# A linear layer with 28 groups of 512 tokens, its weight sums kept for all tokens, and a third recursion level in three of seven products

## The chip, the cores and the metric

The kernel runs on one core of a Trainium2 chip. The metric is the device time of one execution in microseconds (us). Several executions are compared by their median.

## What is computed

Two layers, all in 32-bit floats, each added to its input. x has 32 sequences of 128 tokens and 2048 features.

```python
x = x + (x @ W.T + bias + scale[b] * ((x @ A[b].T) @ B[b].T))   # b = itok_B_1_7, rank 16, 8 adapters
x = x + x @ W1[c].T                                             # c = itok_B_1_14, per sequence, 2048 x 2048
```

The first layer has one weight for all 4096 tokens and a small low-rank term per sequence. The second has a weight per sequence, so that 32 weights of 16 MB are read.

## The kernel before

Both layers multiply by a recursion that replaces 8 products of half-size blocks by 7, at the price of sums of blocks (Strassen's scheme in Winograd's form). In each level the seven products need four sums of x's blocks (s1 to s4) and four of the weight's (t1 to t4), and the results are put together from sums U of the products.

The first layer uses two levels. `PHASES` (lines 21 to 41) writes out the outer one: phase i has a list of x's quarters that are added up, a list of w0's quarters that are added up, the names of an old partial result that it reads and of a new one that it writes ("P1", "U2", "U3", "U4", in DRAM), and for phases 3 to 6 the quarter of the output that becomes final. Within a phase, x is worked on in two groups of 1024 tokens, and w0 in four parts of 256 outputs: a unit is (phase, group, part), 56 in all. Each unit does the inner level: seven products of four matmuls each, 128 x 128 weights on 512 columns of x (`product`, lines 498 to 503, in the order 1, 2, 6, 5, 7, 3, 4), each into one of eight PSUM banks. The sums of w0 are made again for each group: `w_terms` adds the quarters up and `w_sums` makes the inner level's four, one unit ahead. `a_terms` and `a_sums` do the same for x, a group ahead.

All engines run in the order in which the program is written (`manual_schedule`, line 136). ScalarE copies product 1, 6, 5 and 7 out of PSUM, VectorE adds the rest (lines 647 to 691), and `finish` (line 542) adds the old partial result, stores the new one by POOL's queue, or, where the quarter is final, adds x itself (the residual) and the other partial and stores to `x1t`, the second layer's input, in DRAM. `Loads` (lines 45 to 69) hands out slots of one large SBUF tile, `mem`: a load that is in line begins when a slot of its pool is free, and SyncE's queue issues the loads in that order.

The low-rank term has two steps. `lowrank` multiplies x with the adapters' A (32 x 32-wide pieces, side by side in the array) while the quarters of x for phase 1 are in SBUF, and `lowrank_out` scales the result into `low`, with a 1 in an extra row for the bias. `add_low` (line 507) multiplies it with the adapters' B (`load_b`, on POOL's queue) and adds it into the banks of a unit that ends a quarter.

The second layer (lines 698 to 767) takes pairs of sequences and eight parts of the weight per pair, 128 steps n in all. `load_w1` loads two steps ahead, `sums_w1` makes the sums one step ahead (the identity that stands for the residual is added to the weight's diagonal), and seven products of four matmuls follow on 512 columns with 64 rows of tokens (line 732), the first into bank 7. The last unit of the first layer (`ends`, line 640) already loads and adds up for the second.

Of the kernel before, what the change touches and what calls it, by code (L numbers as in the profile page):

```python
# [41 lines left out]
LOW = 1  # L42


class Loads:


    def __init__(self, pools):
        self.free = {k: list(v) for k, v in pools.items()}
        self.todo = []  # L50
        self.held = {}

    def add(self, key, pool, begin):
        self.todo.append((key, pool, begin))

    def pump(self):
        while self.todo and self.free[self.todo[0][1]]:
            key, pool, begin = self.todo.pop(0)
            slot = self.free[pool].pop(0)
            self.held[key] = (pool, slot)  # L60
            begin(slot)
# [4 lines left out]
    def done(self, key):  # L66
        pool, slot = self.held.pop(key)
        self.free[pool].append(slot)
        self.pump()


@with_exitstack
def cond_resid_kernel(
# [55 lines left out]

    nc = tc.nc  # L130
    B, S, D = out.shape
    NW, _, _, _, P, _, _, NF = w1q.shape
    NA, _, _, _, RT, _ = bt.shape
# [10 lines left out]

    mem = const.tile([P, 21, 4 * NF], F32, tag="mem", name="mem")
# [6 lines left out]
    units = [(i, g, o) for i in range(len(PHASES)) for g in range(2) for o in range(4)]  # L152
    part = {
        (k, g, o): dram.tile([P, 4 * NF], F32, tag=f"{k}_{g}{o}", name=f"{k}_{g}{o}")
        for k in ("P1", "U2", "U3", "U4")
        for g in range(2)
        for o in range(4)
# [33 lines left out]
    homes = {"w": (0, 12, 4), "t": [8, 9, 10], "x": (), "s": []}  # L191
# [24 lines left out]
    def sums_w1(n):  # L216
# [14 lines left out]
        )  # L231
        sub(t1, b12, b11)
        sub(b12, b22, b12)
        sub(t2, b22, t1)
        w1s[n] = {1: b11, 2: b21, 3: b22, 4: t4, 5: t1, 6: t2, 7: b12}
        return lambda: sub(t4, b21, t2)
# [25 lines left out]
    with tc.tile_pool(name="c0", bufs=1) as c0, tc.tile_pool(  # L262
        name="ev", bufs=1
    ) as evp, tc.tile_pool(name="bs", bufs=2) as bsp:
        tset = c0.tile([P, 2, 3, 4, P], F32, tag="tset", name="tset")


        low = {
            (r, g): c0.tile([P, 4, S], F32, tag=f"low{r}{g}", name=f"low{r}{g}")
            for r in range(2)  # L270
            for g in range(2)
        }
        bank_a, bank_b, bank_c = ([bank[:, 2 * k + m] for m in range(2)] for k in range(3))
        bank_d, bank_l = banks_r = bank[:, 6], bank[:, 7]


        loads = Loads(
            {"A": range(8), "W": (13, 11, 12), "st": (17, 16, 15, 14, 18)}
        )

        def view(slot, *shape):
            names = "abcd"[: len(shape)]
            return mem[:, slot].rearrange(
                f"p ({' '.join(names)}) -> p {' '.join(names)}", **dict(zip(names[1:], shape[1:]))
            )

        def add_w(n):
            i, g, o = units[n]
            for k, (_, r, c) in enumerate(PHASES[i][1]):
                halves = (0,) if n == 0 else (slice(None),)  # L290
                loads.add(
                    ("W", n, k), "W" if k == 0 else "st",
                    lambda slot, src=w0q[r, c, o], halves=halves: load_w(slot, src, halves),
                )

        def load_w(slot, src, halves):
            for h in halves:
                nc.sync.dma_start(out=view(slot, 2, 2, 4, P)[:, h], in_=src[:, h])  # L298

        def first_a(slot, src):  # L300

            for i in range(2):
                nc.sync.dma_start(out=view(slot, 4, NF)[:, ts(i, 2)], in_=src[:, ts(i, 2)])  # L303
            _, r, c = PHASES[0][1][0]
            load_w(loads.slot(("W", 0, 0)), w0q[r, c, 0], (1,))

        def add_a(group, q):

            i, g = divmod(group, 2)
            t, h = divmod(q, 2)  # L310
            terms = [(r, k) for _, r, k in PHASES[i][0]]
            if i == LOW:
                terms += [(0, 1)]
                loads.add(("a", group, q), "st", lambda slot: load_a(slot, g, t, h))
            for m, (r, k) in enumerate(terms):
                loads.add(
                    ("A", group, q, m), "A" if m == 0 else "st",
                    (lambda slot, src=xq[r, g, t, k, h]: first_a(slot, src))
                    if group == q == 0
                    else lambda slot, src=xq[r, g, t, k, h]: nc.sync.dma_start(  # L320
                        out=view(slot, 4, NF), in_=src
                    ),
                )

        def early(n):

            return n < len(units) and PHASES[units[n][0]][4] and (
                PHASES[units[n][0]][3] or n % 2 == 1
            )

        def add_x(n):
            i, g, o = units[n]

            def load_x(slot):
                r, c, _ = PHASES[i][4]
                for t in range(2):
                    nc.sync.dma_start(
                        out=view(slot, 2, 2, NF)[:, t],
                        in_=xq[r, g, t, c, o // 2, :, ts(o % 2, 2)],
                    )  # L340

            loads.add(("x", n), "st", load_x)

        def add_end(n):
            i, g, o = units[n]
            _, _, old, new, final = PHASES[i]
            if early(n + 1):
                add_x(n + 1)
            if final and not early(n):
                add_x(n)  # L350
            for k in (old, final[2] if final else None):
                if k:
                    loads.add(
                        (k, n), "st",
                        lambda slot, k=k: nc.sync.dma_start(out=mem[:, slot], in_=part[k, g, o]),
                    )

        def load_a(slot, g, t, h):
            for r in range(2):
                for s in range(4):  # L360
                    n = adapter(id0_ok, 16 * r + 8 * g + 4 * t + s, NA - 1, POOL)
                    nc.gpsimd.dma_start(
                        out=view(slot, 2, 4, 8, RT)[:, r, s],
                        in_=at[ds(n, 1), h].rearrange("o p k i r -> (o p) (k i) r"),
                    )

        add_w(0)
        for q in range(2):
            add_a(0, q)
        add_w(1)  # L370
        for q in range(2, 4):
            add_a(0, q)
        for n in range(len(units)):
            if n // 4 + 1 < 2 * len(PHASES):
                add_a(n // 4 + 1, n % 4)
            if n + 2 < len(units):
                add_w(n + 2)
            add_end(n)
        loads.pump()


        for k in range(16):
            nc.tensor.matmul(bank_l[:, :P], lhsT=ident, rhs=ident, start=True, stop=True)

        id0_ok = clamped(id0_sb, NA - 1, "id0_ok")
        id1_ok = clamped(id1_sb, NW - 1, "id1_ok")
# [14 lines left out]
        scale = c0.tile([P, B // 4], F32, tag="scale", name="scale")  # L401


        def signed(sign, dst, src):
            (add if sign > 0 else sub)(dst, dst, src)

        def w_view(n):
            return view(loads.slot(("W", n, 0)), 2, 2, 4, P)

        def w_terms(n):  # L410

            for k, (sign, _, _) in enumerate(PHASES[units[n][0]][1]):
                if k:
                    signed(sign, mem[:, loads.slot(("W", n, 0))], mem[:, loads.slot(("W", n, k))])
                    loads.done(("W", n, k))

        def w_sums(n):

            w = w_view(n)
            t1, t2, t4 = (tset[:, n % 2, k] for k in range(3))  # L420
            sub(t1, w[:, 0, 1], w[:, 0, 0])
            sub(t2, w[:, 1, 1], t1)
            sub(w[:, 0, 1], w[:, 1, 1], w[:, 0, 1])
            sub(t4, w[:, 1, 0], t2)
            return {
                1: w[:, 0, 0], 2: w[:, 1, 0], 3: w[:, 1, 1], 4: t4, 5: t1, 6: t2, 7: w[:, 0, 1]
            }

        def a_terms(group, q):
            terms = PHASES[group // 2][0]  # L430
            dst = mem[:, loads.slot(("A", group, q, 0))]
            for m, (sign, _, _) in enumerate(terms):
                if m:
                    signed(sign, dst, mem[:, loads.slot(("A", group, q, m))])
                    loads.done(("A", group, q, m))
            if group // 2 == LOW:
                loads.done(("A", group, q, len(terms)))
# [104 lines left out]
        def finish(n):  # L542
# [4 lines left out]
            if new:  # L547
# [6 lines left out]
                if old:  # L554
                    loads.done((old, n))
# [282 lines left out]
```

## Time and profile before

| what | us |
|---|---|
| median of 3 runs | 2972.87 (2972.39 to 2975.28) |
| the profiled execution, its own time | 2974.56 |
| its span, first to last instruction | 2972.9 |
| first matmul of the first layer | 7.47 |
| first matmul of the second layer | 1429.81 |

The profile shows one execution. "Busy" is the time in which an engine had an instruction under way. PE is TensorE's matmuls and PEld its weight loads, DVE is VectorE, ACT is ScalarE, POOL is GpSimd, SP is SyncE. A group of instructions is told as line, engine, operation, output<-input, shapes and count, then busy time, mean ns of one, and the engine's idle time ahead of them with what ended it. The sums on VectorE carry the lines of two helpers, 178 (`add`) and 181 (`sub`). A 32-bit matmul of the program shows as two records. DMA issues are told with their size and the median time from issue to landing.

### The profile page before, as it was taken

The page shows a single profiled execution, that of the slowest core. Times are in us where ns is not written, and L with a number is a line of the kernel's source. Part 1 is how long each engine was busy: PE and PEld are TensorE (multiplying, and loading weights), DVE is VectorE, ACT ScalarE, POOL GpSimd, SP SyncE. Part 2 cuts the span into 40 slices and gives each one's busy share as a digit, 9 for nine tenths or more (in the row PEclk, how much of TensorE's full clock was granted, in tenths as well). Part 3 has the DMA queues.
Part 4 walks back from the last instruction along what each step waited for, and adds up shares of the span by engine and source line. Part 5 has one row for each costly group of instructions (what it writes and reads, how often), then busy time and mean ns, then how long its engine had stood idle before and what let it go on. Part 6 is the DMA issues. An engine that isn't in the chain of part 4 may idle for free.

```text
span 2972.9 us, 32939 instructions
## 1 busy us (share of the span) xinstructions
PE 2961.1 (100%) x12384; PEld 1174.1 (39%) x12384; DVE 2351.3 (79%) x1717; ACT 197.7 (7%) x340; POOL 239.1 (8%) x427
## 2 busy tenths in 40 slices
PE   9999999999999999999999999999999999999999
PEld 4445444444444444444333333333333333333333
DVE  3367755567645768874999999999999999999997
ACT  1111111111111111111000000000000000000000
POOL 1111000022212221221000000000000000000000
PEclk9999999999999999999999999999999999999999
DMA  5679866689975899986999999999999999999995
GB/s 226 241 308 357 344 264 255 258 298 346 363 262 210 325 346 377 367 348 234 372 399 383 397 384 406 389 400 388 399 391 396 388 383 408 390 395 387 405 388 222
DMA packets 186015, 1025.62 MB, mean 345 GB/s; under 512 B 23808, under 2 KB 23808, under 8 KB 79616
## 3 DMA queue, kind: packets, MB, share of 16 engines
q1 hardware_dynamic: 142512, 906.68, 77.1%
q0 software_dynamic: 25248, 83.92, 7.4%
q10 hardware_dynamic: 18096, 32.91, 3.5%
q8 instruction: 98, 1.61, 0.2%
q14 instruction: 61, 0.50, 0.0%
HBM read 922.76 MB, written 100.66 MB: 344 GB/s over the span
## 4 chain that ended last, share of the span: by engine, by line
PE 98%; DMA 1%; DVE 1%; issue 0%; SPq 0%; ACT 0%; DVEq 0%; ACTq 0%
PE bank L732 52%; PE bank L500 44%; PE bank L511 1%; PE bank L467 1%; DMA mem<-in_w0q_dram 0%; DMA mem<-in_xq_dram 0%; DVE mem L178 0%; DVE mem L181 0%; DVE tset L181 0%; SPq L303 0%; SPq L298 0%; DVE res L178 0%; ACT p L624 0%; ACT kept L524 0%; DVEq L178 0%
## 5 line engine op out<-in xcount | busy, mean ns | idle before, releaser
L181 DVE TENSOR_TENSOR mem<-mem 128x2048 f32<-128x2048 f32 (+1 forms) x733 | 1483.2, 2052 | 49.6 <-DMA mem<-in_w0q_dram 25.9
L732 PE MATMUL bank<-mem 128*64 128x512 f32 x5120 | 1120.7, 592 | 0.0
L500 PE MATMUL bank<-mem 128*128 128x512 f32 x1792 | 792.4, 595 | 3.1 <-DMA mem<-in_xq_dram 3.1
L732 PEld LDWEIGHTS bank<-mem 128*64 128x64 f32 x5120 | 367.9, 137 | 730.9 <-issue 692.7
L500 PE MATMUL bank<-mem,tset 128*128 128x512 f32 x1344 | 595.8, 593 | 2.5 <-ACT p L624 2.5
L500 PEld LDWEIGHTS bank<-mem 128*128 128x128 f32 x1792 | 340.3, 191 | 425.6 <-issue 420.1
L732 PE MATMUL bank<-mem,s 128*64 128x512 f32 x2048 | 461.2, 592 | 0.0
L178 DVE TENSOR_TENSOR mem<-mem 128x2048 f32<-128x2048 f32 (+2 forms) x195 | 338.9, 1750 | 100.2 <-ACT mem L691 49.0
L500 PEld LDWEIGHTS bank<-mem,tset 128*128 128x128 f32 x1344 | 255.1, 190 | 321.7 <-issue 318.3
L732 PEld LDWEIGHTS bank<-mem,s 128*64 128x64 f32 x2048 | 147.2, 137 | 292.3 <-issue 292.3
L178 DVE TENSOR_TENSOR mem<-u,p 128x512 f32<-128x512 f32 x56 | 38.6, 690 | 197.2 <-ACT u L660 197.2
L492 POOL DMA_DIRECT2D b_sel<-in_bt_dram x256 | 134.7, 526 | 341.7 <-PE bank L511 180.1
L738 ACT COPY pv<-bank 128x512 f32<-128x512 f32 x32 | 18.7, 586 | 1516.1 <-PE bank L732 1041.3
L178 DVE TENSOR_TENSOR pv<-bank,pv 128x512 f32<-128x512 f32 x64 | 44.2, 691 | 78.9 <-PE bank L732 77.9
L178 DVE TENSOR_TENSOR mem<-kept,mem 128x512 f32<-128x512 f32 x28 | 18.7, 690 | 106.4 <-ACT kept L524 106.4
L181 DVE TENSOR_TENSOR tset<-mem,tset 128x512 f32<-128x512 f32 x112 | 77.2, 689 | 7.7 <-PE bank L500 4.1
L178 DVE TENSOR_TENSOR mem<-mem,ident 128x1024 f32<-128x1024 f32 x64 | 78.1, 1220 | 0.0
L178 DVE TENSOR_TENSOR mem<-bank,u 128x512 f32<-128x512 f32 x56 | 38.5, 687 | 48.1 <-PE bank L500 48.1
L535 POOL DMA_DIRECT2D x1t<-mem x64 | 49.0, 770 | 220.3 <-DVE mem L178 216.5
L652 ACT COPY u<-bank 128x512 f32<-128x512 f32 x56 | 32.8, 585 | 357.8 <-PE bank L500 357.8
L691 ACT COPY mem<-bank 128x512 f32<-128x512 f32 x55 | 32.3, 587 | 267.8 <-PE bank L500 255.3
L178 DVE TENSOR_TENSOR mem<-bank,p 128x512 f32<-128x512 f32 x55 | 37.7, 685 | 10.0 <-PE bank L500 6.2
(42 smaller groups left out, 550.9 us busy)
## 6 DMA issues: line engine op xcount, KB each, us to landing
mem<-in_w1q_dram SPq DMA_DIRECT2D x512, 1024.0 KB, 10.4
mem<-in_xq_dram SPq DMA_DIRECT2D x119, 1024.0 KB, 12.9
mem<-in_w0q_dram SPq DMA_DIRECT2D x111, 1024.0 KB, 6.9
mem<-U SPq DMA_DIRECT2D x40, 1024.0 KB, 9.5
mem<-in_xq_dram SPq DMA_DIRECT2D x66, 512.0 KB, 7.8
x1t<-mem POOLq DMA_DIRECT2D x64, 512.0 KB, 8.9
mem<-x1t SPq DMA_DIRECT2D x64, 512.0 KB, 10.2
out_dram<-res ACTq DMA_DIRECT2D x124, 256.0 KB, 6.5
```

What stands on the lines that cost most here:

```text
L178: nc.vector.tensor_tensor(dst, a, b, ALU.add)
L181: nc.vector.tensor_tensor(dst, a, b, ALU.subtract)
L467: nc.tensor.matmul(banks_r[r][ts(s, RT), :S], lhsT=a_sel[:, r, s, 4 * k + i, :], rhs=piece[:, i, s, :], start=(h == 0 and seen[r] == 0 and ...
L492: nc.gpsimd.dma_start(out=b_sel[ts(t, 2 * RT), s], in_=bt[ds(m, 1), c, o].rearrange("o j r m -> (o j r) m"),)
L500: nc.tensor.matmul(dst, lhsT=wts[n][k][:, i, :], rhs=acts[n // 4][k][:, i, :], start=(start and i == 0), stop=(i == 3), skip_group_check=True,
L511: nc.tensor.matmul(dst[:, ts(s, S)], lhsT=b_sels[n][ts(q, RT), s], rhs=low[r, g][ts(q, RT), s], start=(start and s == 0), stop=(s == 3), s ...
L535: nc.gpsimd.dma_start(out=x1t[4 * r + 2 * g + t][:, :, 8 * c + 2 * o : 8 * c + 2 * o + 2].rearrange("s p j m -> p s (j m)"), in_=view(19 + ...
L652: nc.scalar.copy(u2, a)
L691: nc.scalar.copy(zq(z, 1, 0), by_seq(a))
L732: nc.tensor.matmul(dst[ts(j, M)], lhsT=xts[pair, k4 // 2][k][:, j, k4 % 2 * 2 + i], rhs=w1s[n][k][:, j, i], start=(k4 == 0 and i == 0), st ...
L738: nc.scalar.copy(pv[:, 0], dst)
```

## The change

The second layer is the same, but for the slots that it uses and a generator in `sums_w1` that yields where it returned a function. The first layer is written anew:

- Groups have 512 tokens, four per phase, 28 in all, and a group does all 1024 outputs of the phase. So w0's sums are made once per phase and stay for its four groups.
- Products 1, 5, 6 and 7 are done whole (`whole`): four blocks of 128 outputs, four matmuls each, on 256 columns. Products 2, 3 and 4 go through a third level (`third`): seven products of four matmuls on 128 columns. Four sums for x and four for w0 (`third_level`) make their operands, and `third_sums` puts five pieces together on VectorE. Group 0's product 2 is whole.
- The residual of the first layer is an identity that is added to w0's diagonal where w0's quarters are summed (`total` in `w_tasks`), once or twice according to the signs. `finish` doesn't load and add x any more.
- `Tasks` are two lists of VectorE work, for x and for w0, each taken strictly from its head. A turn, seven in a group, hands VectorE work for a credit of 6000 columns, less what it was given otherwise; a task is taken if its loads were begun two turns ago and the products that it must follow are written out. The list for w0 (`w_tasks`) has the same order: totals W, the second level's T1 to T4, the third level's W3. `need` takes all up to a named task at once, and `held` does so until a load has its slot.
- The pools have 10 slots of 8 KB per partition for w0, 9 of 4 KB for x, five for results ("z") and six ("st") for all further terms, partial results and adapters.

The groups' order of work, and the functions that matter for it (shapes of views are left out):

```diff
@@ Loads, Tasks @@
     def pump(self):
-        while self.todo and self.free[self.todo[0][1]]:
...
+            if pool in full or not self.free[pool] or (behind and behind not in self.begun):
+                full.add(pool)
+                rest.append(item)
+                continue
...
+    def ready(self, age):
+        _, _, _, needs, behind = self.todo[0]
+        begun = self.loads.begun
+        return all(k in self.did for k in behind) and all(
+            k in begun and begun[k] + age <= self.loads.now for k in needs
+        )
...
+    def drain(self, budget, age=2):
+        while self.todo and budget > 0 and self.ready(age):
+            budget -= self.step() + 150
+        return budget
+
+    def need(self, *names):
+        for name in names:
+            while name not in self.did:
+                assert self.ready(0), (name, self.todo[0], self.loads.todo[:3], self.loads.free)
+                self.step()
@@ the first layer @@
+        pairs_a = bank[:, 0:2], bank[:, 2:4]
+        pairs_l = bank[:, 4:6], bank[:, 6:8]
...
+                "W": (6, 0, 2, 8, 3, 5, 1, 9, 4, 7), "A": (20, 21, 26, 28, 24, 25, 27, 22, 23),
+                "z": (29, 32, 31, 30, 33), "st": range(34, 40),
...
+        def third_level(work, m11, m12, m21, m22, more, of_x):
+
+            s, u, v = (more[:, k] for k in range(3))
+            if of_x:
+                add(s, m21, m22)
+                sub(u, s, m11)
+                sub(m21, m11, m21)
+                sub(v, m12, u)
+                work.update({1: m11, 2: m12, 3: v, 4: m22, 5: s, 6: u, 7: m21})
...
+            for q in range(4):
+                of_a.add(
+                    ("A", n, q), (len(terms) - 1) * L2, lambda q=q: total(q),
+                    needs=[("A", n, q, m) for m in range(len(terms))],
+                    behind=[("lowrank", n, q)] if i == LOW else [],
+                )
...
+            for k in (1, 2, 3, 4):
+                of_a.add(
+                    ("S", n, k), L2, lambda k=k: inner(k), needs=[("S", n, k)] if k != 3 else []
+                )
...
+                    of_a.add(
+                        ("A3", n, k), L2 + 450, lambda k=k: third(k),
+                        behind=[("PE", n - 1, k)] if n else [],
+                    )
...
+        def held(key):
+
+            while key not in loads.held:
+                task = next((t for t in (of_a, of_w) if t.todo and t.ready(0)), None)
...
+                task.step()
+            return half(loads.slot(key))
...
+        def low_sums(n, j):
+            for t, src in enumerate(low_banks(n)):
+                k = held(("k", n, t, j))
+                add(k, src.rearrange("p b n -> p (b n)"), k)
...
+        def third_sums(n, k):
+            at = 3 * n + k - 2
+            pair, kept, z = pairs_l[at % 2], half(40 + at % 2), z_of(n, *AT[k])
+            upper, c21, c22 = z[:, :NF], z[:, NF : NF + 2 * P], z[:, NF + 2 * P :]
+            add(upper, upper, kept[:, :NF])
+            add(upper, pair[:, 0], upper)
+            add(c22, c22, kept[:, ts(2, 2 * P)])
+            add(c22, c22, kept[:, ts(3, 2 * P)])
+            add(c21, pair[:, 1, : 2 * P], c21)
...
+        def turn(n, spent=0):
+            nonlocal credit
+            loads.now += 1
+            loads.pump()
+            credit = min(credit + 6000 - spent, 8000)
+            credit = of_w.drain(of_a.drain(credit))
...
+        for n, (i, g) in enumerate(groups):
...
+            if n:
+                add(
+                    by_block(z_of(n - 1, 1, 1)),
+                    pairs_a[1 - n % 2].rearrange("p b (k t m) -> p (b k) t m", k=2, t=2),
+                    by_block(z_of(n - 1, 1, 1)),
+                )
+                third_sums(n - 1, 3)
+                of_a.need(("A3", n - 1, 4))
+                of_w.need(("W3", j, 4))
+                spent = 3 * L2
+            of_w.need(("W", i, 0))
+            of_a.need(("A", n, 0))
+            if n:
+                give(n, [(8, 1), (1, 0), (8, 2), (8, 6), (1, 1), (8, 5), (8, 7)])
...
+            if final:
+                add_low(n, 0)
+            if n:
+                spent += finish(n - 1, 1, 1)
+            turn(n, spent)
...
+            if final:
+                low_sums(n, 0)
+            if n:
+                give(n, [(8, 3), (8, 4)])
+            give(n, [(1, 2), (1, 3)])
...
+                spent += finish(n - 1, 0, 1)
+            turn(n, spent)
...
+                third_sums(n - 1, 4)
+                spent += 2 * L2 + finish(n - 1, 1, 0)
+                of_a.need(("A3", n, 2))
+                of_w.need(("W3", i, 2))
+            of_a.need(("S", n, 1))
+            of_w.need(("T", i, 1))
+            parts = mixed(2, 5) if n else [[(2, o) for o in range(4)], [(5, o) for o in range(4)]]
+            give(n, parts[0])
+            turn(n, spent)
+            if lowering:
+                lowrank(n + 1, 0, pair[:, 0, :S])
+            give(n, parts[1])
...
+                third_sums(n, 2)
+            give(n, [(6, o) for o in range(4)])
+            if final:
+                add_low(n, 1)
+            spent += finish(n, 0, 0)
...
+                    [(3, 1), (3, 2), (7, 0), (3, 6), (3, 5), (7, 1)],
+                    [(3, 7), (7, 2), (3, 3), (3, 4), (7, 3)],
...
+        third_sums(n, 3)
+        sums_x1(0, 0)
+        next(sums)
+        third_sums(n, 4)
+        for t, j in ((1, 1), (0, 1), (1, 0)):
+            finish(n, t, j)
```

In a step (k, m), k is the product and m the third level's product or the block of outputs; 8 stands for product 4 of the group before. `mixed` takes product 2's seven steps and product 5's four blocks in turn: (2, 1), (5, 0), (2, 2), (2, 6), (5, 1), (2, 5), (2, 7), and after a turn (5, 2), (2, 3), (2, 4), (5, 3). `lowrank(n + 1, q, ...)` is called four times in the groups 3 to 6, in front of phase 1's groups. Product 2 of group n goes into `pairs_l[3n % 2]`, the pair that `add_low(n, 0)` used before.

## The prediction

> **What bounds the kernel now.** I read the page's busy table first, then the two layers as two windows, then what TensorE waited for, then the groups by form, and last the timeline where a pace was wanted.
>
> ```profile
> PE 2961.1 (100%) x12384; PEld 1174.1 (39%) x12384; DVE 2351.3 (79%) x1717; ACT 197.7 (7%) x340; POOL 239.1 (8%) x427
> ```
>
> The two windows (the first layer ends at 1429.81 us; columns: length, busy time of PE, PEld, DVE, ACT, POOL, clock, DMA share, GB/s):
>
> ```profile
> 0.00:1430.00 1430.00, 1422.91 (x5218) 659.23 (x5220) 914.54 (x856) 179.00 (x308) 237.56 (x425) 1.00 0.79 301
> 1430.00:2973.00 1543.00, 1538.17 (x7168) 514.83 (x7166) 1436.74 (x862) 18.75 (x32) 1.50 (x2) 1.00 0.97 386
> ```
>
> TensorE is full in both; VectorE has 515 us free in the first layer and 106 in the second. TensorE's waits, all of them but the start's:
>
> ```profile
> PE bank L500 <- DMA mem<-in_xq_dram: 3.1, 1, 3.1
> PE bank L500 <- ACT p L624: 2.5, 1, 2.5
> ```
>
> So the first layer is as long as its matmuls. Only fewer columns through TensorE shorten it, as long as nothing else becomes late. The rows by form that I price with:
>
> ```profile
> L500 PE MATMUL bank<-mem 128*128 128x512 f32 x1792 | 792.4, 595 | 3.1 <-DMA mem<-in_xq_dram 3.1
> L181 DVE TENSOR_TENSOR mem<-mem 128x2048 f32<-128x2048 f32 x625 | 1413.1, 2288 | 48.9 <-DMA mem<-in_w0q_dram 25.9 <-PE bank L500 4.4
> L178 DVE TENSOR_TENSOR mem<-mem 128x1024 f32<-128x1024 f32 x64 | 76.0, 1222 | 11.0 <-ACT mem L691 10.5
> L181 DVE TENSOR_TENSOR mem<-mem 128x512 f32<-128x512 f32 x108 | 71.5, 687 | 0.7
> ```
>
> A mean of a matmul is its latency; its pace is read from the timeline (start, length, count):
>
> ```profile
> 6.36 1.09 PEld L383 LDWEIGHTS bank<-ident 128*128 128x128 f32 x9
> 1419.42 7.03 PE L500 MATMUL bank<-mem 128*128 128x512 f32 x16
> 1426.29 3.60 PE L500 MATMUL bank<-mem,tset 128*128 128x512 f32 x8
> ```
>
> Sixteen 512-column records take 1426.29 - 1419.42 = 6.87, so 0.429 us each. The warm-up's records on 128 columns, nine weight loads of 0.19 us, start (1.09 - 0.19)/8 = 0.1125 us apart at full clock, weight load included. A matmul of the program is two records.
>
> **Matmuls.** Removed: 1568 matmuls = 3136 records x 0.4286 = 1344. Added: 28 groups x 4 whole products x 16, and 16 for group 0's whole second product, 1808 matmuls = 3616 records on 256 columns; 83 third-level products x 28 = 2324 matmuls = 4648 records on 128 columns. The latter: 4648 x 0.1115 = 518. No row has 256 columns: half a 512 record (0.214) and two 128 records (0.223) bound it; the line between both shapes gives 0.217, which I take: 785. Sum 1303, **-40** (bounds -51 and -19). `lowrank` and `add_low` issue 1024 records each as before. The columns alone fall by 5.4%, 72 us; the fixed part of short records takes back the rest.
>
> **Start.** Three 0.5 MB loads and the identity's two sums precede the first product, some 2 us later than today; the 3.1 us wait and the half clock behind it (below) go: **-3** (0 to -6).
>
> **VectorE's work.** Counted through the loops: 513 sums on 1024 columns (input sums, second level, residual, U-parts, low rank), 252 on 512, 584 on 256, 28 on 2048, and small ones of 27 us. 256 columns has no row: on the line through the rows of 512 and 1024 it is 0.42 (bounds 0.17, a sum on 8 columns, and 0.69). 513 x 1.22 + 252 x 0.69 + 584 x 0.42 + 28 x 2.29 + 27 = 1136 us, 222 more than today, beside 1370 of TensorE. On the whole it fits. By place it doesn't. A group (512 tokens) is some 46.5 us of TensorE, 48.6 with `add_low`. Its VectorE queue opens with the sum of (1,1) that reads product 7's last bank, which is that group's last matmul. So nothing of the next group's queue starts ahead of that moment T, whatever slack was left. From T: that sum and `third_sums` 3 take 1.2 + 2.6 = 3.9. TensorE from T: five third-level steps of 8 records (5 x 0.89), two blocks of product 1 (2 x 1.74), `add_low` 1.1, then 2 x 0.89 + 2 x 1.74: it wants product 2 at T+14.3 (13.2 without `add_low`), product 5 0.9 later, the sixth step of product 2 another 2.6 later. In front of these stand, in program order:
>
> - Group 20: finish 1.2, S 1.2, two `third` of x 3.4, `low_sums` 1.2, three W sums 3.7, `low_sums` 1.2: its banks are free for product 2 at 15.8 (+1.5). Finish 1.2, `third` 1.7, T1 2.3: product 5 can start at 21.0 (+4.3). T2 to T4, `third_sums`, finish and two steps of W's `third`: 33.1 for the sixth step, wanted at 23.6 (+9.5). 15 us in all.
> - Group 4, the same hand-over of weights: 17.3 for product 5, wanted at 14.1 (+3.2); 28.2 for the sixth step, wanted at 19.9 (+8.3). 11.5.
> - Groups 24 to 27, where x has four terms: 15.2 for product 2 (+0.9), 22.1 for the sixth step, wanted at 18.7 (+3.4). 17 for the four.
> - Groups 14 and 15: two finishes, all of S and two `third` precede `low_sums`: 18.2 for product 2. 8 for both.
>
> Sum 52; independent sums overlap a little (three of 0.69 ran in 1.90), so **+50** (35 to 55).
>
> **Loads.** 232 MB of loads instead of 320, so bandwidth isn't the matter; latency is (issue to landing, KB, us):
>
> ```profile
> mem<-in_xq_dram SPq DMA_DIRECT2D x66, 512.0 KB, 7.8
> U<-mem POOLq DMA_DIRECT2D x24, 1024.0 KB, 10.0
> ```
>
> All terms share six half slots ("st"), a U-part's slot is free only once its store has read it, and `held` makes VectorE free a slot and then needs what is loaded into it. In groups 20 and 24 to 27 the second `low_sums` waits so for its load, with finish, S and `third` queued behind it: 0 to 7.8 less what lies between, about 4 us x 5; groups 12 to 16 some 1 us each: 25. Groups 3 to 6 bring four `lowrank` steps for phase 1. A step needs four half slots, of which the last come free with the sum of the quarter before; TensorE has 5 to 8 us between two steps and the way is 2.4 of sums + 4 to 7.8 of load, with SyncE's queue in order behind it. Some 2 us on each of 12 steps: 25, and the group's other products stand behind each. **+50** (0, if these land early as TensorE's waits show today, to 100).
>
> **Clock.** After the 3.1 us wait at 11 us the granted clock was 0.50 for 6.8 us; after the 2.5 us wait at 1182 us it stayed 1.00:
>
> ```profile
> 13.20:20.00 6.80, 5.86 (x7) 0.50 1.01 426
> 1185.18:1192.00 6.82, 6.82 (x16) 1.00 1.02 423
> ```
>
> So a wait over some 3 us costs about 5.9/2 = 2.9 more, and the ones above are some 12 to 15: **+35** (0 to 45). The Trainium skill, "TensorE: Matmul & The Clock Gate", section "What's actually happening", has the clock halved after an idle window of about 3.4 us until a busy one of that length is over, which speaks against a change that adds such waits and agrees with the row. By the page alone, 15 waits at half rate for 3.4 to 6.8 us would be 25 to 51, an estimate.
>
> **Hand-over.** Layer two's first product writes bank 7. The last `third_sums` of product 4 reads it, behind 1.2 + 2.6 + four x sums (2.6) + a w1 sum (2.3) + its own 2.5 that start 2.6 before TensorE ends: 8.6 us, where today none is lost, and the clock falls: **+11** (5 to 13). Behind it the second layer is the same work: its 1543 us stay, as do its five "t" slots and three w1 slots.
>
> **Off the path.** ScalarE: 20 copies a group; 12 on 256 columns have no row, between 0 and 0.59 (512 columns). At most 12 us of 47, with 0.9 us of other matmuls between a copy and its reader; without that cover 0.6 each. POOL: 4 to 9 issues a group at 0.5 to 0.8. Fewer `b_sel` loads (64 for 256) and no residual load of x (the identity in w0 does it for 13 us of VectorE, counted).
>
> **Sum.** -40 - 3 + 50 + 50 + 35 + 11 = +103. The profiled execution took 2974.56 (span 2972.9), 1.7 over the median of 2972.87; from its own time 3078, against the median 3076. The low bounds together, -51 - 6 + 35 + 0 + 0 + 5 = -17, the high ones -19 + 55 + 100 + 45 + 13 = +194.
>
> **Rivals.**
> - *Only VectorE's queue is late*, the loads land in time: -43 + 50 + 15 (six waits' clock) + 9 = +31, 3006. For it: no load but the first holds TensorE today, and DMA moves less. Against it: six half slots, freed late. Chance 0.25.
> - *VectorE keeps up* (the other side): the sums that TensorE needs at T are done in the group before, because each turn gives VectorE 6000 columns and seven turns are less than a group. Then -43 + 9 leaves 2940. It decides as long as all waits of the first layer with their clock stay under some 30 us, 1 us a group. For it: 1136 of 1370. Against it: the lists above, in program order. Chance 0.15. About no change, between these two, 0.06.
> - *Weight loads pace the 128-column records*: 0.19 instead of 0.1125 gives 4648 x 0.078 = +360, 3340. The warm-up's pace speaks against it: 0.02. By the Trainium skill, same page, "Back-to-back issue gap", pairs of load and matmul on 128 columns run at 81 ns where the stream alone takes 56 (16-bit data); 1.45 times 0.107 (a quarter of a 512 record) would be 0.155 and some +200 us, an estimate that this row contradicts.
>
> **How the numbers follow.** Forecast (queue and loads late) 0.52, the rivals as said. Slower by over 0.2%, about what a measurement of this kernel can tell from no change: 0.52 + 0.25 + 0.02 = 0.79; same 0.06; faster 0.15. The range goes from all low bounds together, 2956 against the median, which takes in no change and leaves out most of the faster case, to all high ones, 3167.
>
> **What would show it.** Right: in the first layer TensorE's records of 256 columns 0.217 apart and of 128 0.1115; VectorE busy 1100 to 1140 us of that layer; TensorE's idle time in front of product 2 and 5 in groups 4, 20 and 24 to 27, released by VectorE, and in front of `lowrank`, released by loads; dips of the clock behind each; the second layer's 1543 us untouched. Wrong: a first layer that ends before 1425 us, or waits on ScalarE's copies inside a third-level product.

## The result and the profile after

The changed kernel takes 3079.95 us (median of 4 runs, 3077.09 to 3082.60) against 2972.95 before: 1.0358 times, 95% interval 1.034 to 1.0376, 107 us slower. The forecast was 3076. The profiled execution took 3082.6 us, with a span of 3080.9. All readings below are from it.

The page's busy table:

```profile
PE 2969.9 (96%) x17512; PEld 1822.6 (59%) x17512; DVE 2509.5 (81%) x2320; ACT 274.7 (9%) x589; POOL 151.5 (5%) x267
```

The two layers as windows (columns as before: length, PE, PEld, DVE, ACT, POOL, clock, DMA share, GB/s). The second layer's first matmul starts at 1534.24 us:

```profile
0.00:1534.24 1534.24, 1429.06 (x10345) 1300.30 (x10345) 1071.38 (x1460) 256.01 (x557) 149.28 (x264) 0.96 0.63 220
1534.24:3080.90 1546.66, 1540.88 (x7168) 522.28 (x7168) 1438.09 (x861) 18.72 (x32) 2.18 (x3) 1.00 0.97 386
```

The first layer ends 104.4 us later, the second takes 3.6 longer (1546.7 for 1543.1). VectorE is busy for 1071 of 1534 us, so it isn't full; and yet TensorE stands. Its waits (total us, times, longest):

```profile
PE bank L714 <- DVE mem L232: 38.3, 10, 8.0
PE bank L714 <- DVE more_w L235: 12.5, 2, 7.3
PE bank L626 <- DMA mem<-in_xq_dram: 12.4, 7, 4.3
PE bank L694 <- DVE mem L235: 10.4, 3, 4.0
PE bank L1021 <- DVE mem L232: 9.0, 1, 9.0
PE bank L626 <- DMA mem<-in_at_dram: 7.8, 3, 4.5
PE bank L714 <- DVE more_a L235: 5.6, 4, 2.7
```

L714 is a third-level step, L694 a whole product, L626 `lowrank`, L1021 the second layer. With four smaller ones, waits of the first layer and its hand-over are 103.8 us: 74.6 on VectorE, 20.2 on loads, 9.0 at the hand-over. Before they were 5.6. The rows by form that the forecast had no row for:

```profile
L694 PE MATMUL bank<-mem 128*128 128x256 f32 x3616 | 854.4, 387 | 11.4 <-DVE mem L235 10.4 <-DVE mem L232 1.0
L714 PE MATMUL bank<-mem 128*128 128x128 f32 x1992 | 268.9, 281 | 40.0 <-DVE mem L232 38.3 <-DVE low L640 1.6
L232 DVE TENSOR_TENSOR mem<-mem 128x256 f32<-128x256 f32 x166 | 69.8, 420 | 2.8
L719 ACT COPY mem<-bank 128x256 f32<-128x256 f32 x332 | 123.6, 372 | 497.0 <-PE bank L714 494.0 <-DVE mem L235 1.7 <-DVE more_a L235 1.0
```

The matmuls did come down. Starts of undisturbed records are 0.216 us apart on 256 columns and 0.1115 on 128, so 3616 x 0.216 + 4648 x 0.1115 = 1299 us stand where 1344 stood. The account of the first layer, 1525.9 us from its first matmul for 1422.3 before: matmuls -45, waits 103.8 - 5.6 = +98, half clock +27 (29.7 in the whole and third-level products, less 2.9), records a little over their pace +7 (some 15 here, some 8 before), and +16 in `lowrank` and `add_low`, which were busy for 40.9 and 39.1 us where they took 29.6 and 34.2. That is +103 of +103.5. Several dips of the clock (stretches at half clock) begin among `lowrank` and `add_low`; what they have of these 16 I didn't split.

**Group 20 in the timeline** (start, length; in brackets the idle time before and what ended it) shows the way from a late load to an idle TensorE:

```profile
1077.70 13.62 SPq L406 DMA_DIRECT2D mem<-U  x4
...
1086.10 1.22 DVE L232 TENSOR_TENSOR mem<-bank,mem 128x1024 f32<-128x1024 f32 x1 [4.36 <-DMA mem<-U]
...
1091.77 1.23 DVE L232 TENSOR_TENSOR mem<-bank,mem 128x1024 f32<-128x1024 f32 x1 [0.79 <-DMA mem<-U]
...
1093.05 2.08 PE L714 MATMUL bank<-mem 128*128 128x128 f32 x8 [6.38 <-DVE mem L232]
...
1095.51 4.61 DVE L235 TENSOR_TENSOR mem<-mem 128x2048 f32<-128x2048 f32 x2
1097.84 3.78 PE L694 MATMUL bank<-mem 128*128 128x256 f32 x8 [2.72 <-DVE mem L235]
...
1109.78 2.04 PE L714 MATMUL bank<-more_a,more_w 128*128 128x128 f32 x8 [7.26 <-DVE more_w L235]
```

The two sums at 1086.10 and 1091.77 are `low_sums`. VectorE itself waits 4.36 and 0.79 us for a U-part that had no half slot in time: the first of them is begun by SyncE at 1077.70, as soon as the `finish` of the group before has given its slot back, and VectorE can read it some 8 us later. Product 2 needs the second sum's banks (6.38). T1 and T2, the 2048-column sums at 1095.51, come only behind all that, and T1 holds product 5 (2.72); T3, T4 and W's third level hold the sixth step (7.26). The waits list puts all three down to VectorE, and the load shows only in VectorE's own idle time.

### The profile page after: what moved, and what is told of

The parts are those of the page before. It is cut to its first block, busy times and chain, and to the rows that moved or that the text cites. A ratio compares the mean times of both kernels' runs of the same rounds, so it can differ in the third digit from the quotient of the medians.

```text
span 3080.9 us, 43798 instructions
## 1 busy us (share of the span) xinstructions
PE 2969.9 (96%) x17512; PEld 1822.6 (59%) x17512; DVE 2509.5 (81%) x2320; ACT 274.7 (9%) x589; POOL 151.5 (5%) x267
## 4 chain that ended last, share of the span: by engine, by line
PE 75%; DVE 9%; issue 9%; DMA 5%; POOL 0%; SPq 0%; POOLq 0%; ACT 0%; DVEq 0%
PE bank L1021 49%; PE bank L694 15%; PE bank L714 10%; DVE mem L232 5%; DVE mem L235 4%; DMA mem<-U 2%; DMA mem<-in_xq_dram 1%; PE bank L665 1%; DMA U<-mem 1%; DMA mem<-in_w1q_dram 1%; PE bank L626 1%; DMA mem<-in_at_dram 1%; DVE more_w L235 0%; DVE more_a L235 0%; POOLq L249 0%
## 5 line engine op out<-in xcount | busy, mean ns | idle before, releaser
L235 DVE TENSOR_TENSOR mem<-mem 128x2048 f32<-128x2048 f32 (+3 forms) x880 | 1522.7, 1758 | 63.1 <-DMA mem<-in_w0q_dram 21.2
L1021 PE MATMUL bank<-mem 128*64 128x512 f32 x5120 | 1123.4, 593 | 9.9 <-DVE mem L232 9.0
L694 PE MATMUL bank<-mem 128*128 128x256 f32 x3616 | 854.4, 387 | 11.4 <-DVE mem L235 10.4
L1021 PEld LDWEIGHTS bank<-mem 128*64 128x64 f32 x5120 | 373.2, 137 | 737.5 <-issue 695.1
L694 PEld LDWEIGHTS bank<-mem 128*128 128x128 f32 x3616 | 678.5, 195 | 97.6 <-DVE mem L235 11.3
L232 DVE TENSOR_TENSOR mem<-mem 128x256 f32<-128x256 f32 (+2 forms) x497 | 419.0, 847 | 175.4 <-ACT mem L700 65.1
L1021 PE MATMUL bank<-mem,s 128*64 128x512 f32 x2048 | 461.4, 592 | 0.0
L232 DVE TENSOR_TENSOR mem<-bank,mem 128x1024 f32<-128x1024 f32 (+2 forms) x259 | 203.6, 794 | 206.1 <-ACT mem L700 137.3
L1021 PEld LDWEIGHTS bank<-mem,s 128*64 128x64 f32 x2048 | 149.1, 137 | 290.4 <-issue 288.4
L714 PE MATMUL bank<-mem 128*128 128x128 f32 x1992 | 268.9, 281 | 40.0 <-DVE mem L232 38.3
L714 PEld LDWEIGHTS bank<-mem 128*128 128x128 f32 x1992 | 256.8, 196 | 55.4 <-DVE mem L232 42.4
L700 ACT COPY mem<-bank 128x512 f32<-128x512 f32 x224 | 131.1, 585 | 770.1 <-PE bank L694 770.1
L714 PE MATMUL bank<-more_a,more_w 128*128 128x128 f32 x1328 | 173.3, 277 | 18.1 <-DVE more_w L235 12.5
L714 PEld LDWEIGHTS bank<-more_a,more_w 128*128 128x128 f32 x1328 | 167.9, 194 | 23.6 <-issue 19.0
L719 ACT COPY mem<-bank 128x256 f32<-128x256 f32 x332 | 123.6, 372 | 497.0 <-PE bank L714 494.0
L714 PE MATMUL bank<-more_a,mem 128*128 128x128 f32 x664 | 89.6, 278 | 0.0
L714 PE MATMUL bank<-mem,more_w 128*128 128x128 f32 x664 | 88.6, 277 | 0.0
L714 PEld LDWEIGHTS bank<-more_a,mem 128*128 128x128 f32 x664 | 85.2, 192 | 4.7
L714 PEld LDWEIGHTS bank<-mem,more_w 128*128 128x128 f32 x664 | 81.7, 194 | 0.0
## 6 DMA issues: line engine op xcount, KB each, us to landing
mem<-in_w1q_dram SPq DMA_DIRECT2D x512, 1024.0 KB, 10.2
```

Source lines behind the costliest of these rows:

```text
L232: nc.vector.tensor_tensor(dst, a, b, ALU.add)
L235: nc.vector.tensor_tensor(dst, a, b, ALU.subtract)
L694: nc.tensor.matmul(dst, lhsT=w[:, m, ts(o, P)], rhs=x[:, m], start=(k in (1, 2, 5) and o % 2 == 0 and m == 0), stop=(m == 3), skip_group_c ...
L700: nc.scalar.copy(by_block(z_of(n, *AT[k]))[:, o - 1 : o + 1], pair[:, o // 2].rearrange("p (k t m) -> p k t m", k=2, t=2),)
L714: nc.tensor.matmul(dst[:, ts(o, P)], lhsT=w[:, f, ts(o, P)], rhs=x[:, f], start=(m in (1, 2) and o == f == 0), stop=(f == 1), skip_group_c ...
L719: nc.scalar.copy(kept[:, ts((1, 6, 7, 5).index(m), 2 * P)], dst)
```

## The experiments

My theory after this result: the terms' half slots are too few. A term's load begins late, so a task isn't "ready" in the turns of the group before, is taken by `need` at the head of the next group's list instead, and there stands between TensorE and its operands. The rivals: VectorE simply has too little credit or throughput; the third level's chains (copy, sum, next product) are too long for any buffering; or the half clock is the larger part.

**One half slot more.** The change has five result slots for "z"; one becomes a seventh "st".

```diff
-                "z": (29, 32, 31, 30, 33), "st": range(34, 40),
+                "z": (29, 32, 31, 30), "st": (*range(34, 40), 33),
```

(Two homes of the second layer's tiles change places with it, so that they are free at the hand-over.)

> One of the five half slots for results ("z") goes to the pool of further terms ("st"), seven instead of six; nothing else, but for the place of two tiles at the hand-over. Theory (waits come from VectorE's queue behind T and, as much, from loads that get their half slot late): loads begin one release earlier, the waits in front of lowrank and of the second low_sums nearly go, with the clock dips behind them: 3000 to 3030. Rival 1 (only the order of VectorE's queue is late, loads land in time anyway): 3065 to 3085. Rival 2 (four result slots are too few, ScalarE's copies wait for stores): over 3085.

Measured: 3048.55, 31 us less than the change. Neither theory's window: the slots matter, but one slot doesn't clear the queue. TensorE's waits of the largest group of the change fall from 38.3 to 6.5, all waits of the first layer and its hand-over from 103.8 to 83.8, while the sums for the third level stay late:

```profile
PE bank L714 <- DVE more_w L235: 16.6, 2, 10.6
PE bank L714 <- DVE more_a L235: 13.5, 5, 6.5
...
PE bank L714 <- DVE mem L232: 6.5, 3, 3.4
```

VectorE's own idle time in front of U-loads fell from 27.8 to 6.0 us.

**More credit for VectorE.**

```diff
-            credit = min(credit + 6000 - spent, 8000)
+            credit = min(credit + 9000 - spent, 12000)
```

> A turn hands VectorE work for 9000 columns instead of 6000 (at most 12000 saved up). Rival 3 (VectorE is handed too little per turn, so that sums which TensorE needs are left for the next group): faster by 20 or more, under 3060. Theory (the sums are not ready to be handed out, for want of loads and of slots that a product must free first, and VectorE can't start ahead of T): no gain, 3075 to 3095.

Measured: 3082.23 (3078.40 to 3086.06), no gain. The credit is not the limit. That the sums left over were not ready to be taken follows from the program and fits; this run alone doesn't show it.

**The last sums in another order.** At the hand-over, `third_sums` of product 4 goes ahead of the second layer's sums.

```diff
         third_sums(n, 3)
+        third_sums(n, 4)
         sums_x1(0, 0)
         next(sums)
-        third_sums(n, 4)
```

> In the last group third_sums of product 4 goes ahead of the second layer's four x sums and one w1 sum. Theory (layer two's first product waits 9.0 for bank 7 behind those): the wait falls to about 4, and with it perhaps the clock dip: 5 to 8 less than the changed kernel, 3072 to 3075. Rival 4 (the second layer's own sums are then late by as much): no difference.

Measured: 3073.47 (3070.31 to 3075.23), 6.5 less. The second layer's first product, in the change and here:

```profile
1534.24 2.04 PE L1021 MATMUL bank<-mem 128*64 128x512 f32 x4 [8.96 <-DVE mem L232]
```

```profile
1521.41 5.35 PE L1021 MATMUL bank<-mem 128*64 128x512 f32 x12 [4.22 <-DVE mem L232]
```

The wait fell by 4.7; another, for u, grew from 0.9 to 2.7. So the time saved is the size of the forecast, but the intervals of the two ratios (1.032 to 1.0354 and 1.034 to 1.0376) overlap, and only the shorter wait is shown.

**No third level at all.** All seven products whole, six half slots as in the change.

```diff
+        TH = ()
...
-            for k in (2, 3, 4):
+            for k in TH:
...
-                    third(n - 1, 4, m)
+                    third(n - 1, 4, m) if 4 in TH else whole(n - 1, 4, m)
```

(The order of the steps, the calls of `need` and the pairs of banks follow: one sum of 1024 columns takes the place of each `third_sums`.)

> The third level is off: products 2, 3 and 4 are whole, with one sum of 1024 columns each; groups of 512, kept weight sums, the identity in w0 and six half slots stay. TensorE's matmuls rise by 55, VectorE's sums fall by some 290. Theory (VectorE's waits at T go, the ones for half slots stay): 3035 to 3055. Rival 5 (the third level's sums and copies make all of the waits): the first layer as long as its matmuls, 2970 to 2990. Rival 1 as rival 5.

Measured: 3049.21 (3049.13 to 3049.29), as expected. The products without third-level sums still wait:

```profile
PE bank L635 <- DMA mem<-in_xq_dram: 18.0, 9, 4.1
PE bank L703 <- DVE mem L232: 17.6, 6, 6.0
```

(L635 is `lowrank`, L703 a whole product.) VectorE waits 39.5 us for U-loads here, more than in the change. So the third level doesn't make all of the waits; but with the same six slots it makes about half of them: TensorE's waits are 48.3 us in place of 103.8, and the kernel is 31 us faster though its matmuls take 55 more.

**The same with eight half slots**: "z" gives none, an extra tile of 8 KB per partition, which the third level's operands left free, holds two more "st".

```diff
+        extra = c0.tile([P, 2, 2 * NF], F32, tag="extra", name="extra")
...
-                "z": (29, 32, 31, 30, 33), "st": range(34, 40),
+                "z": (29, 32, 31, 30, 33), "st": (*range(34, 40), *range(42, 44)),
```

> No third level, and two half slots more for further terms, eight instead of six, in the room that its tiles leave. Beside the same with six, which took 3049. Theory (all that is left there is late half slots and the clock dips behind them): TensorE's waits for lowrank's loads and for low_sums fall from 42 to under 10: 3000 to 3015. Rival (the loads are late by their latency alone, however many slots): 3035 to 3049.

Measured: 3000.03 (2999.50 to 3000.56), 49 less for two slots and nothing else. Of the two groups of waits above, `lowrank`'s is gone and the other is

```profile
PE bank L704 <- DVE mem L232: 1.4, 2, 1.1
```

This settles it for the kernel without a third level: with the arithmetic unchanged, the slots alone take these waits away. Of the +27 that are left over before, 11 are columns (28 x 7 x 32 records of 0.216 us are 1355 for 1344) and 9 are waits (14.9 for 5.6). For the change itself, with its third level, only one slot more was tried.

**Third level in products 3 and 4 only**, product 2 whole (`TH = (3, 4)` in the edit above, product 2 in four blocks of 256 columns), six half slots.

> Product 2 is whole, products 3 and 4 keep the third level; six half slots. TensorE's matmuls rise by 18, VectorE's sums fall by some 96. Theory (product 2 is the one that TensorE wants first after T, so its third-level sums are the late ones): the waits for more_w and more_a, 18, and part of those for S and T go, the waits for half slots stay: 3040 to 3060. Rival (each product's third level costs alike): a third of the way to the kernel without any, about 3070.

Measured: 3032.65 (3030.70 to 3034.60), 47 less than the change, though its matmuls take 18 us more (27 products of 32 records of 0.216 in place of 56 of 0.1115). Both theories missed it on the same side. It takes product 2's `need(("W3", i, 2))` and `need(("A3", n, 2))` away, the third-level sums that stand directly ahead of the product that is late most often. So these sums are a second cause beside the slots, and with six slots not a smaller one.

**Matmuls in the waits.** To separate the idle time from the half clock behind it, 183 matmuls of a tile of zeros are put ahead of eleven of TensorE's waits in groups 4, 14 to 16, 20 and 24 to 26; they add zeros to a bank.

```diff
+                for _ in range(FILL.get((n, k, m), 0)):
+                    nc.tensor.matmul(
+                        pairs_a[n % 2][:, 1, 3 * S :], lhsT=zero, rhs=ident, start=False, stop=True,
+                        skip_group_check=True,
+                    )
```

> The changed kernel, with matmuls by a tile of zeros (they add nothing to a bank that product 1 has left) put into eleven of TensorE's waits in groups 4, 14 to 16, 20 and 24 to 26, each a little shorter than its wait. Theory (a wait over some 3 us costs a half clock behind it, which comes on top of the wait): the dips in these groups go and 10 to 18 with them: 3062 to 3070. Rival (VectorE is the slower one there in any case, so that a slower TensorE only shortens the next wait): 3077 to 3085.

Measured: 3071.92 (3070.17 to 3075.65), 8 less, between the two, with time at half clock down from 113 to 58 us and the mean clock from 0.982 to 0.990. So the dips seem to cost time of their own (the intervals of the two ratios, 1.0321 to 1.0352 and 1.034 to 1.0376, just overlap), but the greater part of the 107 us is the waits.

**The pieces together**: products 3 and 4 only, the hand-over's order, a term taken three turns after its load (age 3), and nine half slots (the one from "z" and two in the extra tile).

```diff
-    def drain(self, budget, age=2):
+    def drain(self, budget, age=3):
...
+        TH = (3, 4)
...
-                "z": (29, 32, 31, 30, 33), "st": range(34, 40),
+                "z": (29, 32, 31, 30), "st": (*range(34, 40), 33, 42, 43),
...
+        third_sums(n, 4)
         sums_x1(0, 0)
         next(sums)
-        third_sums(n, 4)
```

> Products 3 and 4 on the third level, product 2 whole; the half slots that its sums' tiles leave go to the pool of further terms, with one of the result slots: nine instead of six; loads get three turns instead of two; third_sums of product 4 ahead of layer two's sums. Theory (the third level pays as soon as neither the queue behind T nor a half slot is late): TensorE's waits fall under 20 in all, the first layer to 1415 to 1435: 2955 to 2980. Rival (VectorE's total, some 1040 in that layer, is what is late): over 3000.

Measured: 2963.43 (6 runs, 2961.40 to 2965.94), 0.9967 of before, interval 0.9954 to 0.9979: it beats both kernels, the one before by 10 us. The first layer as a window, and TensorE's longest waits:

```profile
0.00:1413.90 1413.90, 1401.96 (x9696) 1266.94 (x9696) 980.34 (x1211) 215.85 (x449) 149.26 (x264) 1.00 0.66 239
```

```profile
PE bank L1034 <- DVE mem L232: 4.2, 1, 4.2
PE bank L724 <- DVE low L650: 2.4, 4, 0.6
```

VectorE waits for no U-load any more. At the same place, group 20, the weights' sums now come ahead of the list that opened the group in the change:

```profile
1002.48 4.62 DVE L235 TENSOR_TENSOR mem<-mem 128x2048 f32<-128x2048 f32 x2
1007.02 1.22 DVE L232 TENSOR_TENSOR mem<-bank,mem 128x1024 f32<-128x1024 f32 x1
...
1014.58 2.35 DVE L232 TENSOR_TENSOR mem<-bank,mem 128x1024 f32<-128x1024 f32 x2 [2.76 <-PE bank L675]
```

T1 and T2 run before the sum of product 7's last bank (1007.02), not behind `low_sums` (now 1014.58, which wait for TensorE, as they should). The number of slots changes the program's order itself, because `ready` asks how many turns ago a load was begun; the age of 3 in this run has a part in that order too.

**Which piece carries it.** Two more runs stand between. All three products on the third level, with seven slots, age 3 and the hand-over's order:

> All three products on the third level, seven half slots for terms, the last sums in the better order, terms taken three turns after their load. Theory (late half slots set the time; the two small edits are worth their own price): 3048.6 of the run with seven slots less 6.5 of the order, and 0 to 25 less for the age of the loads: 3017 to 3045. Rival (the age of the loads is what made the fastest kernel fast): below 2995.

Measured: 3031.84 (3029.09 to 3032.80). And the fastest kernel without its extra tile, so with seven slots:

> The fastest kernel so far without its extra tile: product 2 whole, seven half slots in place of nine. Theory (half slots still set the time between seven and nine): 2985 to 3020, that is 11 to 28 us for each of the last two slots. Rival (product 2 whole and the order were enough, the extra tile does nothing): 2960 to 2975.

Measured: 3009.29 (3008.42 to 3010.64). Here waits on VectorE are back, and VectorE waits 32.6 us for U-loads:

```profile
PE bank L703 <- DVE mem L232: 21.5, 8, 6.0
PE bank L703 <- DVE mem L235: 9.9, 3, 7.0
```

So from the change to the fastest: 3080.0, one slot 3048.6 (-31), order and age 3031.8 (-17), product 2 whole 3009.3 (-22), two more slots 2963.4 (-46). On this way slots are 77 of the 117 us. The shares depend on the way: with six slots product 2 alone gave 47. Nor is VectorE's idle time in front of U-loads a measure of what is lost: with seven slots it was 6.0 us at 3048.6 and 23.0 at 3031.8. All three products on the third level with nine slots wasn't tried: their operands leave no room for the extra tile.

| kernel | us | ratio to before, 95% interval |
|---|---|---|
| the change | 3079.95 | 1.034 to 1.0376 |
| one half slot more | 3048.55 | 1.0233 to 1.0267 |
| more credit | 3082.23 | 1.0347 to 1.0389 |
| hand-over's order | 3073.47 | 1.032 to 1.0354 |
| no third level, six slots | 3049.21 | 1.0236 to 1.0278 |
| no third level, eight slots | 3000.03 | 1.0072 to 1.0109 |
| products 3 and 4, six slots | 3032.65 | 1.0181 to 1.0219 |
| matmuls in the waits | 3071.92 | 1.0321 to 1.0352 |
| all together, nine slots | 2963.43 | 0.9954 to 0.9979 |
| all three products, seven slots | 3031.84 | 1.0182 to 1.0216 |
| products 3 and 4, seven slots | 3009.29 | 1.0109 to 1.0142 |

## Why the prediction was right

The likeliest case came true, 3080 for 3076: VectorE's queue and late loads, with the half clock behind them, cost more than the matmuls save. Three of its six terms hold one by one (matmuls, clock, hand-over), two are right only as a sum, and the start is wrong but small. That the sum lands within 4 us is in part luck: +16 in `lowrank` and `add_low`, which the forecast didn't have, make up for waits and dips that came out smaller than said.

- **Matmuls, -40.** -45. The line between the two shapes gave 0.217 for the 256-column record and it was 0.216; the 128-column one stood in the warm-up's rows. Another +7 went to records a little over their pace, which the forecast didn't have.
- **Start, -3.** Wrong and small: the first product starts 0.9 us later, and the 3.1 us wait has its like in one of 3.7 at 22 us, before product 5, on a sum of the weights, with 3.4 us of half clock.
- **VectorE's queue, +50.** In the groups that it named, the waits are 55.2: 16.4 in group 20 (15 said), 9.2 in group 4 (11.5), 22.7 in 24 to 27 (17), 6.9 in 14 and 15 (8). But part of this is the loads that the next term priced: in group 20 product 2 waited 6.4 for 1.5 said, and the difference is about VectorE's 4.36 + 0.79 for its U-parts. The later waits there were shorter than said (2.7 and 7.3 for 4.3 and 9.5); that TensorE ran at half clock from 1091.3 to 1101.5 and so came later to each product fits, but wasn't separated. Another 19 us stand in groups and places not listed (8, 13, 16, the start, `lowrank`, `add_low`). VectorE was busy for 1071 us of the layer, under the 1100 to 1140 named as a sign: the durations add up to 1145, near the 1136 of the forecast, but one sum can start before the last has ended (a sum of 1.23 us at 1091.77, the next at 1092.91).
- **Loads, +50.** TensorE waits 20 for them directly, all in `lowrank`, for 25 said; the `low_sums` part, 25, is VectorE's 27.8 us of idle time in front of U-loads, and it shows inside the term above. Queue and loads together: 95 for 100. In the median the landing taken was too long: 512 KB took 4.9 us for 7.8 before. Where it mattered it wasn't: the U-part begun at 1077.70 was there some 8 us later. So a late start and a long way came together; what the runs with more slots show is that the earlier start cures it.
- **Clock, +35.** 112 us at half clock in the first layer and its hand-over cost some 30 us in the first layer's products and, behind the hand-over, about 2. The size holds; the rule it was taken from, "a wait over some 3 us", doesn't (last section).
- **Hand-over, +11.** A wait of 9.0, and a second layer longer by 3.6.
- **The step that was too strong** is "nothing of the next group's queue starts ahead of that moment T, whatever slack was left". It held for T1 and T2 in group 20 of the change. But the fastest kernel has T1 and T2 ahead of T: the order isn't set by the sum of (1,1) alone, but by what is ready in the turns before, and so by the slots and the age. The rival "VectorE keeps up" was priced as a matter of VectorE's time and credit; more credit gave nothing, while three slots gave 77 of the 117 us on the way that was tried, and the rest came from product 2 whole, the age and the hand-over's order. The time given for the third rival, 3340, isn't the sum of its terms either: with -43 and +9, as in the second, +360 makes 3300.

The Trainium skill, "Perfetto Trace Analysis", section "Optimization Strategy", says that the same gap repeating on the engine that should be saturated can mean that there isn't enough SBUF for the next tile. Here the gap in front of product 2 repeats in groups 14, 15, 16, 20 and 24 to 27 (3.4, 3.4, 3.6, 6.4, 4.0, 8.0, 3.4 and 1.8 us), and in the kernel with product 2 whole 8 KB more per partition took 46 us away: case and page agree, though the releaser that the profile names is VectorE.

## What to carry to other kernels

A wait that ends with a sum on VectorE isn't yet VectorE's fault: look at what VectorE waited for just before, and behind a load at when its slot came free. Where an order of work is made from "this load was begun so many turns ago", a buffer more or less changes the order, so count the buffers before counting columns. And a saving in matmuls of 3% (45 us here) is more than spent by fifteen waits of 3 to 9 us (74 us here); price the places where two queues meet, not the mean load.

## What the hardware showed beside

**The granted clock falls in steps, and not by the length of the wait alone.** The 18 dips of the first layer and its hand-over last 3.4 (7 times), 6.8 (7) or 10.2 us (4). Three windows of the change, after waits of 2.52, 3.44 and 3.44 us (the clock stands behind POOL's busy time and count):

```profile
480.30:483.70 3.40, 3.28 (x12) 3.01 (x13) 3.40 (x5) 0.37 (x1) 0.53 (x1) 0.50 0.90 365
777.30:784.10 6.80, 6.00 (x20) 5.28 (x21) 6.59 (x12) 0.37 (x1) 1.27 (x2) 0.50 0.56 186
833.70:840.50 6.80, 6.80 (x46) 6.39 (x47) 6.56 (x12) 1.11 (x3) 1.27 (x2) 1.00 0.84 327
```

A wait of 2.52 us halved the clock and one of 3.44 didn't, while another of 3.44 did. So the forecast's "over some 3 us" doesn't hold as a rule.

The trace's record of the granted clock shows why: all 18 dips begin whole multiples of 3.413 us apart, so the clock is set anew at fixed moments, and what counts is how much of a wait falls between two of them. Between 773.84 and 777.25 TensorE was busy for 0.82 us and between 476.88 and 480.29 for 1.02, and a dip followed both times. The other wait of 3.44 us lay across such a moment: busy 1.80 us from 828.45 to 831.87 and 1.58 from 831.87 to 835.28, and no dip. In the change 17 of the 18 dips follow a stretch of 3.41 us with 2.07 us or more of idle TensorE, one (inside `add_low`) a stretch with 1.26; and no stretch of the products at full clock with 1.83 or less idle brought one.

So the same wait can cost a dip in one execution and none in another: in group 15 a wait of 3.43 us fell into a single stretch in the run with the hand-over's order (823.37 to 826.79, busy 0.01), and the clock was 0.50 behind it. The 2.5 us wait of the kernel before, from which the forecast took its rule, was split too (busy 2.10 and 2.19 us of two stretches).

The Trainium skill, "TensorE: Matmul & The Clock Gate", section "What's actually happening", has idle and busy windows of about 3.4 us; the lengths of the dips agree with it; the wait of 2.52 us that brought a dip is shorter than its idle window.

**Short shapes cost their fixed part.** On VectorE a sum on 256 columns took 0.420 us and one on 512 0.687, and on ScalarE a copy of 256 columns 0.372 where one of 512 took 0.585; halving the columns saved a little under four tenths of the time, not half.
